# Batch 2's additions of weighted values: from VectorE to GpSimd

## The chip, the cores and the metric

The kernel runs on one core of a Trainium2 chip. The metric is the device time in microseconds of one execution, as a median over runs; the profile is of one further execution. Engines are named as in the profile: PE is TensorE, DVE is VectorE, ACT is ScalarE, POOL is GpSimd, SP is SyncE, whose queue here issues most transfers.

## The reference

Four sequences (batches 0 to 3) of 512 tokens, width 256, all in float32. The first layer is a cross attention over 1,024 context tokens with 16 heads of 16. The second is a block that attends, for each token, over the batches, and then runs a mixture of experts. Cut to what matters here, with the third-batch step marked:

```python
x = x + xattn(layernorm(x), ctx, ctx, mask, ...)          # 4 x 512 x 256
hidden = layernorm(x)
qkv = einsum('sbh,oh->sbo', layernorm(hidden) * w1 + b1, qkv_weight)   # 16 heads of q, 4 of k and v
scores = einsum('sbhd,tbhd->bhst', q, k) * 0.25
probs = softmax(where(causal, scores, min))
attn = einsum('bhst,tbhd->sbhd', probs, v)                # <- the sum over t
h2 = hidden + attn @ proj_weight.T
gate = softmax(layernorm(h2) @ router_weight.T)           # top 2 of 8 experts
out = x + h2 + sum over the two chosen experts of gate * gelu(. @ w1) @ w2
```

The block's first axis, over which it attends causally, is what the first layer calls the batch. So token s of batch b attends to token s of batches 0 to b: for batch 2 the sum over t has three terms, each a weighted copy of one batch's values.

## The kernel before

**Stages.** First come some 28 us of loading and preparation, then to about 637 us the cross attention of 16 groups (4 batches by 4 groups of 4 heads), with the second layer's work on batches 0, 1 and 2 spread between its steps, and then the experts' tiles (39 of them) with batch 3's second layer between them.

**Cross attention.** A group takes 8 steps. In each step TensorE forms score products twice: `psm` (L1147), from which DVE takes maxima, `mx` (L1154), ten steps ahead, and `pss` (L1168), from which ACT takes exponentials, `ex` (L1176). `ex` meets the values in `av` (L1186), which a group sums in one PSUM bank over its 8 steps. At the end of a group DVE's transposition to `oraw` (L862) empties that bank, so the next group's first `av` waits for it. `divide` then makes `rec` and `on` (L875, L876) and every second time `onT` (L862).

**Second layer.** `half(b, h)` is a generator that does two of the four 128-token tiles of batch b, one piece at a time; pieces end at a `yield`. For batch 2, in order: variances and their power on POOL (L268); normalised rows `hn` (L434, DVE); `hT`; `q`, `keys`, `values` (L455 to L458); POOL's products `pr` of q with the keys of batches 0, 1 and 2 (L489); sums, maxima and exponentials in `sc` (L500 to L509); then one piece with the weighted values: POOL writes batch 0's product into `at` and those of batches 1 and 2 into `pr[:, 1]` and `pr[:, 2]` (L514; the profile calls this buffer `pv`), and two additions put them onto `at` (L532). That piece ends, and at least two steps later the transposes `psa` (L294) read `at`, followed by `aT`, `psp` (L542), `h2` (L549), statistics, `vm` (L555), its power `rm` on POOL, `xt` on POOL (L557), Newton's step `sm`, `sm`, `rm` (L274 to L276) and `rows` (L562) on DVE, the transposes `psx`, and the router.

**Order.** The order of instructions is written out: each engine runs its own instructions in the order in which the program issues them, and one that waits holds all behind it on that engine. Which step a piece falls into is decided by a planner from costs given with each piece (`PARTS`); those costs don't depend on the engine that line 532 names. Buffers of the step: `at` and `pr` have one buffer each for batches 0 to 2, all in SBUF, float32, 128 x 512 a piece.

Line 532 names DVE for batch 2 and POOL for batch 1. Batch 0 has nothing to add, and batch 3 sums with one reduction (L525) instead.

Of the kernel before, what the change touches and what calls it, by code (L numbers as in the profile page):

```python
# [10 lines left out]
ALU = mybir.AluOpType  # L11
# [162 lines left out]
def kernel(  # L174
# [21 lines left out]
    nc = tc.nc  # L196
# [207 lines left out]
    def products_of(name, b):  # L404
        if b < B - 1:
            return k2.tile([P, B - 1, HALF, DK], F32, tag="pr", name=name, bufs=1)
        return late["pool"].tile([P, B, HALF, DK], F32, tag="prlast", name=name, bufs=2)
# [6 lines left out]
    def half(b, h):  # L414
# [47 lines left out]
        def of_batch(kv, j):  # L462

            return (
                kv[j][:, t0 : t0 + 2, :]
                .rearrange("p t (k d) -> p (t k) d", d=DK)
                .unsqueeze(2)
                .to_broadcast([P, 2 * KVH, REP, DK])
            )

        def grouped(x):
            return x.rearrange("p (k r) d -> p k r d", r=REP)

        if b == 0:

            yield
            yield
            yield
            at = k2.tile([P, HALF, DK], F32, tag="at", name=f"at{n}", bufs=1)
            nc.gpsimd.tensor_copy(grouped(at), of_batch(values, 0))  # L480
            yield
        else:

            def engine(j):
                return nc.vector if last and j % 2 else nc.gpsimd

            pr = products_of(f"pr{n}", b)
            for j in range(b + 1):
                engine(j).tensor_tensor(  # L489
                    grouped(pr[:, j]),  # L490
                    grouped(q.rearrange("p i (h d) -> p (i h) d", d=DK)),
                    of_batch(keys, j),
                    ALU.mult,
                )
            yield "D1.5|G2.4"
            sc = k2.tile([P, B, HALF], F32, tag="sc", name=f"sc{n}")[:, 0 : b + 1, :]
            top = k2.tile([P, HALF], F32, tag="top", name=f"top{n}")
            by_head = sc.rearrange("p j n -> p n j")
            over = [P, b + 1, HALF]
            nc.vector.tensor_reduce(sc, pr[:, 0 : b + 1], AX.X, ALU.add)  # L500
            nc.vector.tensor_reduce(top, by_head, AX.X, ALU.max)
            nc.vector.tensor_tensor(sc, sc, top.unsqueeze(1).to_broadcast(over), ALU.subtract)
            if last:
                yield "D3!"
            nc.scalar.activation(sc, sc, AF.Exp, scale=SCALE)
            yield "A2.9"
            nc.vector.tensor_reduce(top, by_head, AX.X, ALU.add)
            nc.vector.reciprocal(top, top)
            nc.vector.tensor_tensor(sc, sc, top.unsqueeze(1).to_broadcast(over), ALU.mult)  # L509
            yield "D1"  # L510
            at = k2.tile([P, HALF, DK], F32, tag="at", name=f"at{n}", bufs=1)
            pr = products_of(f"pv{n}", b)
            for j in range(b + 1):
                engine(j).tensor_tensor(  # L514
                    grouped(pr[:, j] if j or last else at),
                    of_batch(values, j),
                    sc[:, j, :]
                    .rearrange("p (k r) -> p k r", r=REP)
                    .unsqueeze(3)
                    .to_broadcast([P, 2 * KVH, REP, DK]),  # L520
                    ALU.mult,
                )
            if last:
                yield "D1.5|G2.4"
                nc.vector.tensor_reduce(  # L525
                    at.rearrange("p n d -> p (n d)"),
                    pr.rearrange("p j n d -> p (n d) j"),
                    AX.X,
                    ALU.add,
                )  # L530
            for j in range(1, 1 if last else b + 1):
                (nc.vector if b == 2 else nc.gpsimd).tensor_tensor(at, at, pr[:, j], ALU.add)  # L532
            yield "D2.2!"
        aT = wide(f"aT{n}")
        rows_of = at.rearrange("p (i h) d -> p i (h d)", i=2)
# [349 lines left out]
    def project_o(b, t):  # L885
# [9 lines left out]
        nc.vector.tensor_tensor(xt[:, b, t, :], ps[:, 0:D], xt[:, b, t, :], ALU.add)  # L895

    halves = {(b, h): half(b, h) for b in range(B) for h in range(2)}

    with ExitStack() as actx:
# [35 lines left out]
        for h in range(H):  # L935

            g, j = divmod(h, 4)
# [776 lines left out]
```

## Time and profile before

| | us |
|---|---|
| Median of 3 runs (836.19 to 838.76) | 836.48 |
| The profiled execution's own time | 840.55 |
| Its span, first to last instruction | 838.8 |
| Mean granted TensorE clock | 0.985 |
| DVE's four instructions of L532: shortest, median, longest | 0.692, 0.898, 1.529 |
| POOL's two instructions of L532 (batch 1): shortest, longest | 1.268, 1.273 |
| POOL's product `at` of L514: shortest, longest | 1.043, 1.053 |
| POOL's `xt` of L557, an addition of the same size: mean | 1.266 |
| DVE's `on` of L876: shortest, median, longest | 0.424, 0.425, 1.232 |

Each row of a timeline has the start in the span, the length, the engine, the line, the operation, the output and input by the program's names, their shapes, and how many instructions were merged into the row. In square brackets stands how long the engine had been idle before it, and what ended that. A granted clock of 0.5 means that TensorE ran at half its full speed. Windows give the busy time of each engine in a stretch. Batch 2's two halves reach line 532 at 584.6 us and 611.1 us.

### The profile page before, as it was taken

The numbers are of one execution on the slowest core, as the hardware profiler recorded it, in microseconds if no ns is written. First come the engines' busy times: TensorE is split into PE (matmuls) and PEld (weight loads), VectorE is DVE, ScalarE is ACT, GpSimd is POOL, SyncE is SP. The second block draws the span as 40 slices with busy tenths as digits, with TensorE's granted clock in tenths as the row PEclk, the third lists the DMA queues.
The fourth block names the chain that finished last, engine by engine and source line by source line (L and its number), as shares of the span: only waits on it lengthen the run. The fifth ranks groups of instructions, "written<-read, shape, count | busy, mean of one in ns | idle before, by whom it ended". The sixth has DMA issues, their size and how long they took to land.

```text
span 838.8 us, 14851 instructions
## 1 busy us (share of the span) xinstructions
PE 791.9 (94%) x5255; PEld 409.2 (49%) x5255; DVE 561.7 (67%) x1335; ACT 441.9 (53%) x896; POOL 290.0 (35%) x445
## 2 busy tenths in 40 slices
PE   5999999999999999999999999999989989789993
PEld 4553433333433333444433333433326878789992
DVE  5687667666778777887786878888845587501033
ACT  2326666655565656555655565555555665434441
POOL 6815351001353300154653201223223564525531
PEclk9999999999999999999999999999989999989997
DMA  7229203408000000000000006000071450278954
GB/s 234 60 92 312 63 1 109 126 1 233 2 26 1 1 1 2 1 27 27 2 1 1 1 1 202 27 20 8 1 254 58 141 190 20 78 241 268 342 175 152
DMA packets 55641, 73.36 MB, mean 87 GB/s; under 512 B 5721, under 2 KB 40569, under 8 KB 55568
## 3 DMA queue, kind: packets, MB, share of 16 engines
q1 hardware_dynamic: 49968, 61.08, 23.8%
q0 software_dynamic: 4080, 10.07, 3.3%
q10 hardware_dynamic: 1520, 1.27, 0.5%
q8 instruction: 42, 0.69, 0.3%
q14 instruction: 31, 0.25, 0.1%
HBM read 42.88 MB, written 30.75 MB: 88 GB/s over the span
## 4 chain that ended last, share of the span: by engine, by line
PE 69%; DVE 11%; issue 10%; POOL 7%; DMA 1%; ACT 1%; POOLq 0%; ACTq 0%; SPq 0%; DVEq 0%
PE psm L1147 29%; PE av L1186 13%; PE psv L1061 4%; POOL given_rows L1483 4%; PE psk L1028 3%; DVE mx L1154 3%; PE pss L1168 3%; PE psq L448 2%; PE psp L542 2%; PE psy L1469 2%; PE psqt L1127 2%; PE pskt L1049 2%; PE psp L888 2%; PE psu L1451 2%; PE psq L1107 1%
## 5 line engine op out<-in xcount | busy, mean ns | idle before, releaser
L1154 DVE TENSOR_REDUCE mx<-psm 128x1 f32<-128x512 f32 x512 | 326.1, 683 | 115.2 <-PE pss L1168 100.7
L1176 ACT ACTIVATE ex<-pss 128x512 f32<-128x512 f32 x512 | 277.4, 596 | 203.6 <-PE pss L1168 192.4
L1147 PE MATMUL psm<-kT_odd,shared 32*128 32x512 f32 x512 | 152.1, 639 | 3.1 <-ACT shared L1135 2.1
L1168 PE MATMUL pss<-qt,shared 32*128 32x512 f32 x512 | 151.6, 639 | 0.0
L1168 PE MATMUL pss<-qt,kT_odd 32*128 32x512 f32 x512 | 146.5, 646 | 0.9 <-ACT ex L1176 0.9
L1147 PE MATMUL psm<-shared 32*128 32x512 f32 x512 | 143.0, 639 | 0.7 <-ACT shared L1135 0.7
L1186 PE MATMUL av<-ex,vaug 128*32 128x512 f32 (+1 forms) x888 | 107.1, 551 | 4.4 <-DVE sm L274 4.1
L1451 PE MATMUL psu<-shared 128*128 128x128 f32 x624 | 78.2, 277 | 2.9 <-ACT shared L1436 2.4
L993 POOL TENSOR_TENSOR shared<-shared 128x256 f32<-128x256 f32 x44 | 33.5, 761 | 135.0 <-ACT shared L1036 113.6
L1147 PEld LDWEIGHTS psm<-kT_odd,shared 32*128 32x128 f32 x512 | 43.8, 183 | 74.3 <-DVE mx L1154 33.8
L1451 PEld LDWEIGHTS psu<-shared 128*128 128x128 f32 x624 | 76.6, 193 | 6.9 <-ACT shared L1436 4.0
L1469 PE MATMUL psy<-shared 128*128 x312 | 77.6, 393 | 1.1 <-issue 0.6
L1147 PEld LDWEIGHTS psm<-shared 32*128 32x128 f32 x512 | 42.3, 183 | 65.5 <-DVE mx L1154 29.2
L1469 PEld LDWEIGHTS psy<-shared 128*128 128x128 f32 x312 | 58.0, 196 | 9.4 <-issue 1.7
L1186 PEld LDWEIGHTS av<-ex,vaug 128*32 128x32 f32 x888 | 17.8, 108 | 89.2 <-issue 81.2
L1460 ACT ACTIVATE shared<-psu 128x512 f32<-128x512 f32 x39 | 23.4, 599 | 49.2 <-PE psu L1451 22.7
L1168 PEld LDWEIGHTS pss<-qt,kT_odd 32*128 32x128 f32 x512 | 42.8, 184 | 8.3 <-ACT ex L1176 3.8
L995 POOL TENSOR_TENSOR shared<-shared 128x128 f32<-128x128 f32 x88 | 44.8, 530 | 0.0
L1168 PEld LDWEIGHTS pss<-qt,shared 32*128 32x128 f32 x512 | 43.6, 183 | 2.0 <-ACT ex L1176 1.5
L268 POOL TENSOR_TENSOR rm<-vm,power 128x2 f32<-128x2 f32 x8 | 5.7, 712 | 109.4 <-DVE vm L555 87.0
L653 POOL DMA_INDIRECT table<-rows,index x32 | 32.4, 1013 | 31.9 <-issue 11.4
L1515 DVE SCALAR_TENSOR_TENSOR y<-y,gate,xt 128x256 f32<-128x256 f32 x16 | 7.7, 481 | 45.9 <-DMA y<-given_rows 45.9
(296 smaller groups left out, 1041.4 us busy)
## 6 DMA issues: line engine op xcount, KB each, us to landing
shared<-in_moe_w_dram SPq DMA_DIRECT2D x47, 512.0 KB
table<-zeros SPq DMA_DIRECT2D x8, 2120.0 KB
shared<-in_ctxT_dram SPq DMA_DIRECT2D x8, 512.0 KB
y<-given_rows SPq DMA_DIRECT2D x12, 256.0 KB
shared<-table SPq DMA_DIRECT2D x18, 132.5 KB
xt<-in_x_dram SPq DMA_DIRECT2D x4, 512.0 KB
rows_d<-table SPq DMA_DIRECT2D x13, 132.5 KB
out_dram<-y SPq DMA_DIRECT2D x6, 256.0 KB
```

What stands on the lines that cost most here:

```text
L653: inst = nc.gpsimd.indirect_dma_start(out=table, out_offset=bass.IndirectOffsetOnAxis(ap=index, axis=0), in_=rows, in_offset=None, bounds_ ...
L993: engine.tensor_tensor(a, src, over(f[:, 0:DK]), ALU.mult)
L995: engine.tensor_tensor(r[:, :, i::2], src[:, :, 1 - i :: 2], over(f[:, DK + i : 2 * DK : 2]), ALU.mult,)
L1061: nc.tensor.matmul(ps[:, 0:D], context(b, kc, c), wv_sb[:, c, :], start=(c == 0), stop=(c == KC - 1),)
L1147: nc.tensor.matmul(ps, q1[m][rows, t * P : (t + 1) * P], kT[b % 2][rows, g, h * 512 : (h + 1) * 512], start=True, stop=True,)
L1154: nc.vector.tensor_reduce(mx[m][:, t, j, h : h + 1], ps, AX.X, ALU.max)
L1168: nc.tensor.matmul(ps, kT[b % 2][rows, g, kc * P : (kc + 1) * P], q2[m][rows, :], start=True, stop=True,)
L1176: nc.scalar.activation(ex[m, kc, j], ps, AF.Exp, scale=SCALE)
L1186: nc.tensor.matmul(av[m][32 * j : 32 * j + 32, over], vaug[(b * NKC + kc) % VRING][:, 4 * g + j, :], x[:, over], start=(kc == 0), stop=(kc ...
L1451: nc.tensor.matmul(ps_of[k][:, of], w1_of[k][:, c, of], xT_of[k][:, c, :], start=(c == 0), stop=(c == KC - 1),)
L1469: nc.tensor.matmul(ps_of[k], h_of[k][:, f * P : (f + 1) * P], w2_sb[:, bass.ds(weights_of[k] + f * D, D)], start=(f == 0), stop=(f == F // ...
L1483: inst = nc.gpsimd.indirect_dma_start(out=given_rows[n], out_offset=bass.IndirectOffsetOnAxis(ap=number[name][:, i, :], axis=0), in_=y, in ...
```

## The change

Line 532 chose the engine by the batch. Now it always takes POOL, which also writes the three products that are added. So for batch 2, four additions of 128 x 512 float32 (two in each half) go from DVE's queue to POOL's, right behind the products of line 514. Nothing else differs: the planner's costs, the steps of the pieces, the buffers and all other instructions are as before, and DVE has no instruction left in that piece.

```diff
@@ half(b, h)
             for j in range(1, 1 if last else b + 1):
-                (nc.vector if b == 2 else nc.gpsimd).tensor_tensor(at, at, pr[:, j], ALU.add)
+                nc.gpsimd.tensor_tensor(at, at, pr[:, j], ALU.add)
             yield "D2.2!"
```

## The prediction

> **What bounds the kernel now.** I read the page first, then the answer for line 532, then the timeline around its four VectorE instructions, the chain of waits there, and windows of TensorE's clock.
>
> The page says TensorE is the engine that sets the span, but that is an average: the change touches four instructions of batch 2, so what counts is which wait ends last near 585 and 611 us.
>
> ```profile
> span 838.8 us, 14851 instructions
> PE 791.9 (94%) x5255; PEld 409.2 (49%) x5255; DVE 561.7 (67%) x1335; ACT 441.9 (53%) x896; POOL 290.0 (35%) x445
> ```
>
> The answer for line 532 shows the moved instructions (four on DVE), the same addition already on POOL for batch 1 (1.27 us each), and one long DVE wait.
>
> ```profile
> L532 DVE TENSOR_TENSOR at<-at,pv x4: 692/898/1529, 584.6 to 612.7; 128x512 f32<-128x512 f32 x4
> L532 POOL TENSOR_TENSOR at<-at,pv x2: 1268/1270/1273, 447.8 to 476.0; 128x512 f32<-128x512 f32 x2
> ...
>   POOL pv L514: 4.1, 1
> ```
>
> Timeline, half (2, 0): start, length, engine, line.
>
> ```profile
> 583.06 2.06 POOL L514 TENSOR_TENSOR pv<-values,sc 128x512 f32<-128x512 f32 x2
> 584.56 1.90 DVE L532 TENSOR_TENSOR at<-at,pv 128x512 f32<-128x512 f32 x2
> 586.61 3.90 POOL L489 TENSOR_TENSOR pr<-q,keys 128x512 f32<-128x512 f32 x3 [1.49 <-DVE keys L457]
> 586.92 1.23 DVE L876 TENSOR_TENSOR on<-oraw,rec 128x256 f32<-128x256 f32 x1
> 588.83 2.44 DVE L1154 TENSOR_REDUCE mx<-psm 128x1 f32<-128x512 f32 x4
> 589.53 0.69 PE L1147 MATMUL psm<-kT_odd,shared 32*128 32x512 f32 x1 [0.96 <-DVE mx L1154]
> ```
>
> DVE works without a pause; the chain of waits runs down DVE from 583.38 to the variance `vm` at 606.98, and TensorE waits 0.96 us for it. So DVE is the bound here, not TensorE. Half (2, 1):
>
> ```profile
> 607.06 0.72 POOL L268 TENSOR_TENSOR rm<-vm,power 128x2 f32<-128x2 f32 x1 [16.55 <-DVE vm L555]
> 607.77 1.26 POOL L557 TENSOR_TENSOR xt<-xt,h 128x512 f32<-128x512 f32 x1
> 609.00 1.04 POOL L514 TENSOR_TENSOR at<-values,sc 128x512 f32<-128x512 f32 x1
> 610.01 2.05 POOL L514 TENSOR_TENSOR pv<-values,sc 128x512 f32<-128x512 f32 x2
> 611.09 2.33 DVE L532 TENSOR_TENSOR at<-at,pv 128x512 f32<-128x512 f32 x2 [4.11 <-POOL pv L514]
> 613.33 0.71 DVE L862 STREAM_TRANSPOSE oraw<-av 128x512 f32<-128x512 f32 x1
> 614.09 1.94 PE L1186 MATMUL av<-ex,vaug 128*32 128x512 f32 x8 [4.08 <-DVE sm L274]
> 615.96 1.12 PE L294 MATMUL psa<-ident,at 128*128 128x128 f32 x4
> ```
>
> Here DVE stands 4.11 us at the first addition, and `oraw`, which frees the bank that the next `av` products need, stands behind it in DVE's order; so TensorE stands 4.08 us. Its clock drops (columns PE, PEld, DVE, ACT, POOL busy, then granted clock, DMA share, GB/s):
>
> ```profile
> 608.00:614.00 6.00, 2.01 (x16) 0.34 (x12) 2.81 (x4) 4.13 (x8) 4.06 (x4) 0.82 0.66 210
> 614.00:620.00 6.00, 5.91 (x29) 1.72 (x30) 1.73 (x8) 1.56 (x4) 0.00 (x0) 0.61 0.90 272
> ```
>
> In half-microsecond windows it is 0.50 from 611.8 to 618.7, so 4.6 us of work from 614.09 run at half speed: some 2.3 us lost.
>
> **The change, first half.** It takes 1.90 us from DVE at 584.56. Only 0.69 + 0.69 is work; the rest is DVE held until POOL's current instruction ends: the first addition ends at 585.67, the products at 585.12. `on` shows the same: 1.23 us beside POOL's `pr`, against a median of 0.42. POOL gets two additions of 1.27 with 0.08 before each (the gap after the product in batch 1: 447.71 to 447.79): 585.20 to 586.47 and 586.55 to 587.82. DVE goes on to `keys` once ACT's copy of `q` ends (584.87 + 0.37 = 585.24), then `values` and `rec`, and reaches `on` near 585.8. It is held to the end of the first addition, 586.47, and ends 0.27 later (as before: POOL's first `pr` ended at 586.61 + 1.27 = 587.88, `on` at 588.15). So 586.74 instead of 588.15: DVE is **1.4 us** early, and as the chain is DVE's alone to 606.98, all that follows is too: TensorE, which waited for `mx` at 589.53, moves by as much. Ends for it: 0.1, if `on` gets through only after both additions (587.82 + 0.27 = 588.09); 1.9, if all the addition time is saved. I take 1.4, by the row of `on`, which got its turn with two `pr` instructions still to come.
>
> What waits for POOL now: the three `pr` behind the additions start 587.9 instead of 586.61 and end by 591.8. Line 500 wants them at 600.05 - 1.4 = 598.6: 6.8 us of cover. `psa` of this half stood at 593.64, less 1.4 is 592.2, against 587.82: 4.4 us of cover. Both would cost, microsecond for microsecond, only beyond that. SP's queue has nothing of this step, and the step issues no DMA.
>
> **Second half**, first in the old times. POOL's row is `rm`, `xt`, three products, which end at 612.06, then additions 612.14 to 613.41 and 613.49 to 614.76. Meanwhile DVE no longer stands: `av` of the old product ends at 608.94, `oraw` at 609.7, the `ex` that the next `av` reads at 610.08, so `av` runs at 610.1 to 611.2 instead of 614.09 to 616.03. Then TensorE meets `psa`, which needs the additions: the stall moves from `oraw` to `at`. DVE's `sm`, `sm`, `rm`, two `rows` and `on` now fall beside POOL's products and additions. What this costs POOL: at 253.5 to 257.1 eight such short DVE instructions, `hn` (0.41 alone, 0.6 to 0.9 there) among them, lay beside POOL's and left those at their usual lengths; three `pr` took 3.90 beside `on` against 3.73 without. I take 0.15. Ends: 0, and 2.0, if each of the two later products and two additions grows by the 0.45 to 0.51 that the longest rows show in batch 3 (1.50 against 1.04, 1.77 against 1.26). So `psa` comes at 614.76 + 0.15 + 0.05 (step from engine to engine) = 614.96 instead of 615.96: **1.0 us** early, and with the 1.4 before it 2.4. DVE's `rows` are needed by `psx` only after `psa`, `pss` and `av`, over 2 us later; late by more, they would hold that. Behind POOL's additions its next instruction is `rm` at 628.8: 14 us of cover.
>
> **The clock** is the third term. TensorE's stall is now 611.2 to 614.96, 3.8 us against 4.08, with dense work before and after. Before, the clock fell 1.8 us after the stall began. I count the same 2.3 us lost, difference 0; ends +2.3 gained (no drop) and 1.1 lost (all 6.8 us of the slow stretch fall on work: 3.4 - 2.3).
>
> The Trainium skill ("TensorE: Matmul & The Clock Gate", "HAM oscillation") has idle gaps above some 3.4 us halve the clock, by a free-running window; the trace's drop, 1.8 us into a gap, doesn't need a whole idle window. By the page a gap of 3.8 us would mostly escape, and the sum would be 831.8; by the row it is 834.1.
>
> The Trainium skill ("SBUF — State Buffer", "Who interferes with whom") speaks against the change: a VectorE instruction with two SBUF inputs and a GpSimd one that reads SBUF exclude each other, whoever comes second waiting for the whole instruction. The held `on` agrees; GpSimd's unlengthened rows at 254 to 258 us don't. If POOL waited for all 1.7 us of those DVE instructions, the sum would be 835.6 and not 834.1.
>
> **Sum.** After 616 us TensorE is busy without a gap to 638, then the experts and batch 3 hang on its results; the rows read for the first tiles were asked for from 607.5 to 623.7 and are used from 637, so DMA doesn't absorb the gain, and the 6.6 us wait for rows of the last list near 734 follows DVE's and POOL's work. So 840.55 (the profiled execution, span 838.8) less 2.4 gives 838.15; that execution lies 4.07 above the median of the runs, so for the median 836.48 - 2.4 = **834.1**. Own range 832.9 to 835.4.
>
> **Rivals.**
> - *No cold clock* in the second half: 834.1 - 2.3 = 831.8. For it: the stall is shorter and split from the one before by `av`. Against: by 0.3 us only.
> - *The first half gives nothing*: `on` is held through both additions, gain 0.1 + 1.0 = 1.1, so 835.4. For it: POOL's additions follow without a wait. Against: `on` slipped in between two `pr`.
> - *Slower*: POOL pays for the port. At line 532 of half (2, 1), POOL's four instructions grow to 2.0 us more, `psa` comes at 616.81, 0.85 late; less 0.1 from the first half, and with up to 1.1 of cold clock on top: 837.2 to 838.3. It decides from the point where POOL's lengthening exceeds the first half's gain by 1.15. For it: batch 3's rows. Against: those stand beside DVE instructions of 0.69 us, here they are mostly 0.16.
> - *It doesn't do what it says*: excluded, since the trace has this very line on POOL in batch 1.
>
> **How the numbers follow.** Forecast 0.56, no cold clock 0.15, first half nothing 0.16, slower 0.13. 0.3% is 2.5 us, about what a measurement of this kernel can tell. Faster than 833.97 are a little under half of the forecast, whose middle lies 0.1 us above that (0.27), the clock case (0.15) and a clock gain on top of the second rival (0.02): 0.44. Slower than 838.99 needs the slower case and more: 0.10. The rest, 0.46, is within. The range 831.6 to 836.9 reaches to the clock case and leaves most of the slower one out.
>
> **What would show it.** Line 532 has six POOL rows of 1.27 and none on DVE; `on` of half (2, 0) ends 1.4 us earlier after POOL's products than now; no DVE wait of 4 us near 611; `av` runs before `psa` with the stall between them; `psa` follows POOL's last addition within 0.1 us. I am wrong if `psa` stands later relative to `vm` than 9.0 us (now 615.96 - 606.98), if POOL's additions take over 1.6 us, or if the 2.4 us gained by 616 are gone at 742.

## The result, and the profile after

| | before | after |
|---|---|---|
| Median of 12 runs each, us | 837.32 (834.66 to 838.80) | 839.49 (837.19 to 841.66) |
| Ratio of times | | 1.0032 [1.0020, 1.0044] |
| Profiled execution, us | 840.55 | 840.89 |
| Its span, us | 838.8 | 839.0 |
| Mean granted TensorE clock | 0.985 | 0.981 |

The change made the kernel slower by 0.32% by the ratio, about 2.7 us (the two medians lie 2.2 apart). 834.1 had been forecast, 2.4 us below the 836.48 of the runs known then, in a range of 831.6 to 836.9. The table's last three rows already hold a hint: the two profiled executions differ by 0.3 us only, and by the clock.

The page of the changed kernel: DVE lost four instructions, POOL got four, and POOL's busy time rose by 4.9 us.

```profile
span 839.0 us, 14850 instructions
PE 792.5 (94%) x5255; PEld 409.6 (49%) x5255; DVE 563.2 (67%) x1331; ACT 442.0 (53%) x896; POOL 294.9 (35%) x449
```

DVE's line speaks: four instructions worth 4 us are gone, yet it is busy 1.5 us *longer*. Other DVE instructions became slower, in both halves. The answer for line 532 shows the edit in place, six instructions on POOL of 1.25 to 1.34 us, and who waits for them:

```profile
L532 POOL TENSOR_TENSOR at<-at,pv x6: 1252/1270/1336, 448.1 to 616.3; 128x512 f32<-128x512 f32 x6
...
  PE psa L294: 3.5, 1
```

**First half of the change**, the timeline of DVE, POOL and TensorE around it, in the changed kernel:

```profile
583.72 1.05 POOL L514 TENSOR_TENSOR at<-values,sc 128x512 f32<-128x512 f32 x1 [13.36 <-DVE sc L509]
584.73 2.06 POOL L514 TENSOR_TENSOR pv<-values,sc 128x512 f32<-128x512 f32 x2
586.75 2.69 POOL L532 TENSOR_TENSOR at<-at,pv 128x512 f32<-128x512 f32 x2
587.77 0.53 DVE L876 TENSOR_TENSOR on<-oraw,rec 128x256 f32<-128x256 f32 x1
588.97 2.45 DVE L1154 TENSOR_REDUCE mx<-psm 128x1 f32<-128x512 f32 x4
589.51 3.73 POOL L489 TENSOR_TENSOR pr<-q,keys 128x512 f32<-128x512 f32 x3
591.34 0.70 DVE L693 SCALAR_TENSOR_TENSOR lna<-base,base 128x8 f32<-128x8 f32 x1
592.07 1.31 DVE L682 TENSOR_TENSOR gea<-lna,full 128x128 f32<-128x128 f32 x1
594.54 2.48 DVE L1154 TENSOR_REDUCE mx<-psm 128x1 f32<-128x512 f32 x4
595.37 0.63 PE L294 MATMUL psa<-ident,at 128*128 128x128 f32 x4 [1.65 <-DVE mx L1154]
```

And the same instructions in the kernel before:

```profile
582.05 1.05 POOL L514 TENSOR_TENSOR at<-values,sc 128x512 f32<-128x512 f32 x1 [12.00 <-DVE sc L509]
...
591.20 0.14 DVE L693 SCALAR_TENSOR_TENSOR lna<-base,base 128x8 f32<-128x8 f32 x1
591.38 0.29 DVE L682 TENSOR_TENSOR gea<-lna,full 128x128 f32<-128x128 f32 x1
...
592.82 2.47 DVE L1154 TENSOR_REDUCE mx<-psm 128x1 f32<-128x512 f32 x4
593.64 0.63 PE L294 MATMUL psa<-ident,at 128*128 128x128 f32 x4 [0.18 <-DVE mx L1154]
```

`lna` and `gea` belong to a piece that plans the list of rows for the first expert tiles. They have nothing to do with the second layer; they only happen to come next on DVE. In the old kernel POOL's three `pr` were over at 586.61 + 3.90 = 590.51, and `lna` came 0.69 us behind them. Now the two additions stand ahead of `pr`, which run from 589.51 to 593.24, and `lna` and `gea` fall among them. `lna` takes 0.70 in place of 0.14 and `gea` 1.31 in place of 0.29: together **1.58 us**, as much as DVE had been relieved of. The maxima `mx` behind them are late, and TensorE, which stood 0.18 us at `psa`, stands 1.65.

All of this timeline lies some 1.7 us later than in the old profile for a reason of its own: POOL's first product `at` starts at 583.72 and not 582.05, behind a stretch at half clock near 580 that comes before the first changed instruction. So intervals are compared here, not places: the products end at 586.79 and `on` at 588.30, 1.51 apart, where it was 585.12 to 588.15, 3.03 apart.

**What the stall brings.** Windows of the changed kernel (start:end length, busy time and instructions of PE, PEld, DVE, ACT and POOL, granted clock, DMA share, GB/s):

```profile
590.00:596.00 6.00, 4.35 (x46) 1.62 (x38) 5.79 (x13) 2.87 (x6) 3.24 (x3) 1.00 0.00 1
596.00:602.00 6.00, 6.00 (x28) 2.02 (x28) 4.72 (x17) 2.57 (x5) 0.00 (x0) 0.72 0.01 3
```

The first of them in the kernel before:

```profile
590.00:596.00 6.00, 5.82 (x48) 2.10 (x48) 5.70 (x19) 3.46 (x7) 0.51 (x1) 1.00 0.02 4
```

TensorE is busy 4.35 of 6 us in place of 5.82, and in the next 6 us the clock is 0.72: it is 0.50 from 596.1 to 599.5 and 1.00 after. TensorE has work throughout (6.00 busy), so the 3.41 us at half clock cost half of that, 1.7 us. All stretches at half clock that the profiles of this case show are 3.41 us long, or two or three times that, but for the last, which begins near 830 us and runs past the end. Their mean number in an execution, in units of 3.41 us, can therefore be read from its mean clock: (1 - clock) x span / 1.7. For the changed kernel's 12 runs that gives 8.2; for the before runs beside the experiments below, 6.2 to 6.7.

**Second half**, in the changed kernel:

```profile
609.99 0.72 POOL L268 TENSOR_TENSOR rm<-vm,power 128x2 f32<-128x2 f32 x1 [16.75 <-DVE vm L555]
...
611.96 0.72 DVE L862 STREAM_TRANSPOSE oraw<-av 128x512 f32<-128x512 f32 x1 [2.05 <-PE av L1186]
...
612.82 1.24 PE L1186 MATMUL av<-ex,vaug 128*32 128x512 f32 x8
613.03 0.98 DVE L275 TENSOR_TENSOR sm<-sm,rm 128x2 f32<-128x2 f32 x1
...
614.96 2.59 POOL L532 TENSOR_TENSOR at<-at,pv 128x512 f32<-128x512 f32 x2
615.05 2.65 DVE L562 TENSOR_SCALAR rows<-h,mvm,rm 128x256 f32<-128x256 f32 x2
...
617.61 1.11 PE L294 MATMUL psa<-ident,at 128*128 128x128 f32 x4 [3.55 <-POOL at L532]
...
620.67 1.94 PE L1186 MATMUL av<-ex,vaug 128*32 128x512 f32 x8
```

This went as forecast: no DVE wait of 4 us, `av` before `psa`, the stall between them, `psa` 0.06 us behind POOL's last addition. From the start of `rm` to `psa` are 7.62 us, where it was 615.96 - 607.06 = 8.90: 1.28 us less. But where the `av` of the old kernel took 1.94 us, all of it at half clock (1.07 at full), now an `av` *behind* the stall takes 1.94, and the one before it 1.24. In this execution the slow stretch was moved, not removed.

### The profile page after: what moved, and what is told of

It is laid out like the page before. It is cut to its first block, busy times and chain, and to the rows that moved or that the text cites. A ratio compares the mean times of both kernels' runs of the same rounds, so it can differ in the third digit from the quotient of the medians.

```text
span 839.0 us, 14850 instructions
## 1 busy us (share of the span) xinstructions
PE 792.5 (94%) x5255; PEld 409.6 (49%) x5255; DVE 563.2 (67%) x1331; ACT 442.0 (53%) x896; POOL 294.9 (35%) x449
## 3 DMA queue, kind: packets, MB, share of 16 engines
q10 hardware_dynamic: 1520, 1.27, 0.5%
## 4 chain that ended last, share of the span: by engine, by line
PE 69%; DVE 9%; issue 8%; POOL 6%; DMA 3%; SPq 2%; ACT 2%; ACTq 0%; POOLq 0%; DVEq 0%
PE psm L1147 29%; PE av L1186 14%; PE psv L1061 4%; PE psk L1028 3%; PE pss L1168 3%; POOL given_rows L1483 3%; DVE mx L1154 2%; PE psq L448 2%; PE psp L542 2%; PE pskt L1049 2%; PE psqt L1127 2%; PE psp L888 2%; PE psu L1451 2%; PE psq L1107 1%; PE psy L1469 1%
```

## The experiments

The theory at the outset: the first half's gain is taken back by `pr` falling on `lna` and `gea`, and the stall this makes brings half clock. Rivals: the second half costs more than it saves; the two sets of runs differ by chance; the half clock is the whole loss and has nothing to do with the stall at `psa` of half (2, 0).

All ratios are to the kernel before, run alternately on the same chip. "Half-clock stretches" are means over an execution, counted as above.

**Before, unchanged**, to see what no change looks like.

> The kernel before under another label, so that its own runs, with their mean granted clocks, stand beside those of the others. All theories: no difference beyond 0.1%. If the time of single runs goes with the granted clock, a run whose mean clock is 0.004 lower should be some 3 us longer.

Measured: 837.15 us, 1.0006 [0.9996, 1.0015], 6.4 half-clock stretches. The loss of 0.32% is five times this difference, and a second set of the changed kernel, further down, is slower too, so chance between sets is not the reason. Among single runs the time does go with the clock: a line through these 12 runs gives 2.6 us for 0.004 of mean clock, one through the 35 before runs beside them 1.8, where 3 had been expected. So a stretch in the count costs some 0.9 to 1.3 us on average, less than 1.7, since not every stretch lies on work.

**One half of the change alone.** On the kernel before:

```diff
-(nc.vector if b == 2 else nc.gpsimd).tensor_tensor(at, at, pr[:, j], ALU.add)
+(nc.vector if b == 2 and h == 1 else nc.gpsimd).tensor_tensor(at, at, pr[:, j], ALU.add)
```

moves the first half's alone; with `h == 0` in place of `h == 1` the second half's alone.

> Additions on POOL in half (2, 0) only. Collision theory (POOL's pr of the next half comes 1.3 us later and then stands beside DVE's lna and gea, which take 1.6 us more): slower by 1 to 3 us, with lna and gea near 0.7 and 1.3 us. Rival (the moved stall before psa in half (2, 1) costs the time): same as before or 1.4 us faster. Rival (chance of the clock windows): no difference.

> Additions on POOL in half (2, 1) only. Collision theory: faster by about 1 us (psa follows vm after 7.7 us and not after 9.0), lna and gea at 0.14 and 0.29 us. Rival (the moved stall before psa costs the time, by a longer slow clock): slower by 1 to 3 us. Rival (chance): no difference.

Measured: first half alone 839.49, 1.0023 [1.0008, 1.0037], 7.5 stretches; second half alone 836.90, 1.0001 [0.9991, 1.0012], 6.5. The loss is the first half's; the rival that puts it on the second falls. The one profile of the first half alone caught a mild case: `lna` took 0.58 and `gea` 0.29, since `gea` got in between two of POOL's instructions, and TensorE stood 0.6 at `psa`. So the same kernel was run once more:

> The first-half-only kernel again. Slower than before by 0.1 to 0.35%. If the loss comes by slow windows: mean clock lower than before's by 0.002 or more, the rest of the time within 0.5 us of before's.

Measured: 838.35, 1.0015 [1.0001, 1.0029], 7.0 stretches, and this time the whole picture:

```profile
590.07 0.69 DVE L693 SCALAR_TENSOR_TENSOR lna<-base,base 128x8 f32<-128x8 f32 x1
590.79 1.32 DVE L682 TENSOR_TENSOR gea<-lna,full 128x128 f32<-128x128 f32 x1
```

with a wait of 1.8 us at `psa`, and in the windows half clock directly behind it:

```profile
589.00:595.40 6.40, 4.64 (x42) 1.85 (x40) 6.20 (x13) 2.89 (x6) 2.96 (x3) 1.00 0.00 1
595.40:599.00 3.60, 3.60 (x18) 0.79 (x18) 3.15 (x14) 1.20 (x2) 0.00 (x0) 0.56 0.02 5
```

The second half alone shows why its gain of 1.28 us comes to nothing in the time. Its windows, split where the clock falls:

```profile
609.00:615.50 6.50, 3.01 (x23) 0.98 (x20) 5.84 (x8) 3.59 (x8) 5.99 (x6) 1.00 0.75 229
615.50:619.00 3.50, 3.50 (x19) 0.75 (x17) 0.34 (x1) 1.72 (x4) 0.00 (x0) 0.53 0.95 285
```

The stretch at half clock lies wholly on work (3.50 busy of 3.50), where in the profile of the kernel before it began during the stall. A fair interval runs from the power `rm` of half (2, 0) to the same `rm` of half (2, 1), compared between profiles with the same number of half-clock stretches inside. With one stretch it is 21.20 to 21.22 us with the additions on DVE (three profiles) and 20.79 to 20.87 on POOL (three profiles): 0.4 us gained, not 1.0. With none, in runs with filled stalls below, 19.65 against 19.25: again 0.4. With two it is 21.76 to 21.86 on DVE (three profiles, the kernel before among them) and 21.89 and 22.12 on POOL (the change, and the change with its first stall filled): nothing gained. There the pair began some 2.2 us before the stall's end in the old order, and 0.6 to 1.0 before it in the new, so more of it fell on work. A ratio known to 0.1% can't tell 0.4 us from nothing.

**The colliding piece one step later.** If the theory holds, the changed kernel with `lna` and `gea` out of the way must keep the first half's gain. In the planner's steps, on the changed kernel and, for what the move does by itself, on the kernel before:

```diff
 steps = plan.spread(START, END)
+lists_at = [T for T in range(START, END) for f, args in steps[T] if args[:1] == (first_list,)]
+piece = [s for s in steps[lists_at[0]] if s[1][:1] == (first_list,)][0]
+steps[lists_at[0]].remove(piece)
+steps[lists_at[0] + 1].insert(0, piece)
```

> The changed kernel, with the first piece of the list's planning (lna, gea and the six small instructions behind them on DVE) put one step later, behind the next four maxima. Collision theory: lna and gea at 0.14 and 0.29 us, and faster than before by 1 to 3 us. Rival (stall before psa): still slower than before by about 2 us, as the change is. Rival (chance): no difference.

> The kernel before, with only the planning piece put one step later as in the list-later run. Collision theory: lna and gea are short in both, so within 0.7 us of before. Rival (the later piece is a gain of its own, whatever the additions do): faster than before by 1 to 2 us, as the list-later run was against the change.

Measured: changed kernel with the piece later 836.05, 0.9987 [0.9974, 1.0001], 7.3 stretches; the kernel before with it 839.32, 1.0010 [0.9996, 1.0024], 6.7. In the first, `pr` were over at 592.86, and then:

```profile
593.89 0.16 DVE L693 SCALAR_TENSOR_TENSOR lna<-base,base 128x8 f32<-128x8 f32 x1
594.09 0.29 DVE L682 TENSOR_TENSOR gea<-lna,full 128x128 f32<-128x128 f32 x1
```

Out of POOL's way they take 0.16 and 0.29, as in the kernel before (0.14 and 0.29), and the loss is gone; the later place brings the kernel before nothing. No stretch follows `psa` of half (2, 0) in this profile. But the count of 7.3 is above the 6.2 of the before runs beside it: the loss went without a lower count, and where those stretches lie in the other executions is open. The interval that tells it best runs from POOL's first product of half (2, 0) to `rm` of that half, through DVE's whole chain: 25.01 us before (582.05 to 607.06) and 24.16 here (583.34 to 607.50). With the piece later and the additions on DVE it was 25.70; with the piece later and the additions on POOL, 24.17 in the filled run below. So against the same place of the piece the first half is worth 1.5 us, close to the 1.4 forecast.

**POOL later, additions left where they were.** On the kernel before, two instructions of like length on POOL behind `pr`:

```diff
+if (b, h) == (2, 1):
+    nothing = named["zeros"][:, 0:1].unsqueeze(2).to_broadcast([P, HALF, DK])
+    for _ in range(2):
+        nc.gpsimd.tensor_tensor(pr[:, 0], pr[:, 0], nothing, ALU.add)
```

> The kernel before (all four additions on DVE), with two more POOL additions of zero onto one piece of pr behind the three pr products of half (2, 1): the result stays the same, POOL stays busy 2.5 us longer, to about 593. Collision theory: lna and gea take about 0.7 and 1.3 us and not 0.14 and 0.29, and the kernel is slower than before by 1.5 to 3.5 us, with no addition moved. Rival (the loss lies in what the moved additions themselves do): within 0.5 us of before.

Measured: 839.39, 1.0012 [0.9998, 1.0026], 6.6 stretches: some 1 us slower, less than the collision theory expected and more than its rival did. The expected collision hardly came about:

```profile
591.37 2.29 POOL L498 TENSOR_TENSOR pr<-pr,zeros 128x512 f32<-128x512 f32 x2
592.09 0.34 DVE L697 SCALAR_TENSOR_TENSOR lna<-base,base 128x8 f32<-128x8 f32 x1
592.47 0.29 DVE L686 TENSOR_TENSOR gea<-lna,full 128x128 f32<-128x128 f32 x1
```

`lna` waited 0.2 us, and `gea` slipped in ahead of the second instruction of POOL; only a later one, `lha` at 593.11, took 0.57 in place of 0.17. This run decides nothing, except that how long DVE is held depends on where within POOL's instruction it arrives.

**The stalls filled.** If half clock follows TensorE's stalls, transposes whose result nobody reads, put into a stall, should keep the clock up and change nothing else. Into the stall at `psa` of half (2, 1), in the changed kernel and in the one with the piece later:

```diff
-def transposed(dst, src, name, weight=None):
+def transposed(dst, src, name, weight=None, fill=0):
...
+    for _ in range(fill):
+        nc.tensor.transpose(ps[:, 0:P], ident, ident)
...
+fill = 20 if (b, h) == (2, 1) else 0
-transposed(aT, lambda i: rows_of[:, i, :], f"psa{n}")
+transposed(aT, lambda i: rows_of[:, i, :], f"psa{n}", fill=fill)
```

> The changed kernel, with 20 transposes of the identity (3.1 us at full clock) into psa's bank ahead of its own transposes in half (2, 1): TensorE works through its stall. If the slow clock behind this stall is part of the loss: one to two slow windows of 3.4 us fewer there, mean clock up by 0.002 to 0.004, 1.5 to 3.5 us faster than the change. If the collision alone is the loss: no faster than the change by more than 0.5 us.

> The changed kernel with the planning piece one step later and the 20 transposes in the stall. If both terms are real and add up: 832 to 834.5 us, faster than before by 2 to 4 us. If the clock term is not real: about the list-later run, 836.

Measured: the change filled 837.39, 0.9986 [0.9970, 1.0003], 5.8 stretches; with the piece later too 836.44, **0.9969 [0.9958, 0.9981]**, 6.1 stretches, by its ratio the fastest version of all here, on a chip whose before runs had a median of 838.68 and 6.7 stretches. The transposes took 2.40 us, so that TensorE still stood 1.19 at `psa`. The clock holds, in the changed kernel filled:

```profile
610.00:616.00 6.00, 4.81 (x40) 2.77 (x36) 5.52 (x6) 3.44 (x7) 5.87 (x6) 1.00 0.72 236
616.00:622.00 6.00, 6.00 (x44) 2.43 (x44) 1.17 (x4) 4.23 (x9) 0.00 (x0) 1.00 0.81 256
```

That it pays in the old order too is shown by the kernel before with its own stall filled, ahead of the first `av` of the last group, which waits for its bank:

```diff
 av[m] = pso.tile(...)
+if m == M - 1:
+    work = pss.tile([P, 512], F32, tag="s", name="work")
+    for _ in range(22):
+        nc.tensor.transpose(work[:, 0:P], ident, ident)
```

> The kernel before, with 22 transposes of the identity (3.5 us) into a score bank ahead of the first av of the last group, where TensorE stands 4.1 us. If the slow clock behind this stall cost the kernel before as much as I put it at (2.3 us): 1.5 to 2.5 us faster than before. If the stall's slow clock is a cost of the change alone: no difference.

Measured: 835.67, 0.9983 [0.9973, 0.9992], 1.4 us and so a little less than expected, 6.0 stretches, and a clock of 1.00 where the kernel before had 0.61:

```profile
614.00:620.00 6.00, 4.45 (x35) 1.61 (x34) 3.49 (x10) 1.89 (x5) 0.00 (x0) 1.00 0.89 263
```

One thing here doesn't fit well. With the second half's stall filled in both, the change (0.9986) and the kernel before (0.9983) are equal within their intervals, though the first half's stall is not filled in either. By the plain change's 1.0018 to 1.0032 some 0.2 to 0.3% should have been left; put the other way, this fill brought the change 0.3 to 0.5%, and the kernel before 0.17. The intervals, on two chips, are too wide to exclude 0.2%.

**The stall that the change made, filled.** The sharpest test of the last rival: transposes into the stall at `psa` of half (2, 0), which leave the collision alone, beside the plain change on the same chip.

```diff
+if (b, h) == (2, 0):
+    work = pss.tile([P, 512], F32, tag="s", name="work")
+    for _ in range(10):
+        nc.tensor.transpose(work[:, 0:P], ident, ident)
 transposed(aT, lambda i: rows_of[:, i, :], f"psa{n}")
```

> The changed kernel, with 10 transposes of the identity (1.6 us) into a score bank ahead of psa in half (2, 0), where TensorE stood 1.65 us behind the delayed maxima. If the slow window at 596 us is part of the loss in most executions: none there, mean clock up by 0.001 to 0.002, 0.8 to 1.7 us faster than the change. If that window was one execution's chance: as the change, within 0.5 us.

> The changed kernel once more, beside the others of this call. Slower than before by 0.2 to 0.45%, some two slow clock windows more per execution than before (mean clock lower by 0.003 to 0.004). Its profile shows lna and gea near 0.7 and 1.3 us again, psa 7.7 us behind vm, and whether 596 us has a slow window again.

Measured: filled 837.32, 1.0000 [0.9990, 1.0009]; plain 839.13, 1.0018 [1.0007, 1.0028]. So the slow clock behind this one stall is 0.18% of the time, 1.5 us (by the single times of the two sets the 95% interval of the difference is 0.5 to 2.6 us), which is the whole loss of this set. The collision stays in the filled run:

```profile
589.70 0.69 DVE L697 SCALAR_TENSOR_TENSOR lna<-base,base 128x8 f32<-128x8 f32 x1
590.42 1.31 DVE L686 TENSOR_TENSOR gea<-lna,full 128x128 f32<-128x128 f32 x1
```

but the clock doesn't fall behind it (the transposes took 1.31 us, and TensorE still stood 0.51 at `psa`):

```profile
590.00:596.00 6.00, 5.49 (x50) 2.68 (x46) 5.71 (x15) 2.73 (x6) 1.59 (x2) 1.00 0.01 4
596.00:602.00 6.00, 6.00 (x40) 2.35 (x39) 5.79 (x15) 1.71 (x4) 0.00 (x0) 1.00 0.00 0
```

The mean number of half-clock stretches is 6.7 against 7.8 for the plain change on the same chip, and 6.3 for the kernel before. The profiles say the same in the interval from POOL's first product of half (2, 0) to `rm`:

| | us | stretches at half clock inside |
|---|---|---|
| additions on DVE, planning piece in its place (four profiles) | 25.00 to 25.36 | none |
| on POOL, full collision: stall filled; only the later stall filled | 25.07; 25.07 | none |
| on POOL, full collision: the change; first half again | 26.27; 26.43 | one |
| on POOL, full collision: the change again | 27.82 | two |
| on POOL, piece later (two profiles) | 24.16, 24.17 | none |

With the clock held, what the first half saves on DVE and what `lna` and `gea` lose are equal; a slow stretch adds 1.2 to 1.4 us. The second row's latter run had nothing put into this stall, so it isn't the transposes that bring 25.07.

## Why the prediction was wrong, step by step

**What held.** Six POOL rows of 1.27 and none on DVE. `on` 1.5 us earlier against POOL's products (1.51 behind them, 3.03 before; 1.4 forecast). No 4 us wait on DVE, `av` ahead of `psa`, `psa` 0.06 us behind the last addition, and 617.61 - 609.91 = 7.70 us behind `vm`, where more than 9.0 would have been wrong. The rival in which POOL pays for the port did not come: the two additions beside DVE's `rm` and `rows` took 2.59 together, next to twice 1.27.

**The step that failed: "What waits for POOL now".** It asked who needs the delayed `pr`, found line 500 with "6.8 us of cover" and `psa` with 4.4, and put the delay at nothing. Both covers were real. But `pr` is also a neighbour. It ran 1.23 us later behind POOL's products (2.72 in place of 1.49) while DVE ran 1.5 earlier, so the two engines moved some 2.6 us against one another, and `lna`, which had come 0.69 us after the end of `pr` (591.20 - 590.51), now came 1.90 ahead of it (593.24 - 591.34). Price 1.58 us, which is the whole of the "**1.4 us** early". That it is this is shown by the piece moved one step on (durations back to 0.16 and 0.29, 1.5 us of gain in the interval), and by the two runs in which the collision is full and no slow clock follows (25.07 us, no gain left). The prediction had used this very mechanism for the old `on`, and missed it in the place to which it was moved.

The Trainium skill ("SBUF — State Buffer", "Who interferes with whom") has a VectorE instruction with two SBUF inputs locked out for the whole GpSimd instruction that it meets, and the other way round. DVE's side agrees with `lna` (0.14 to 0.70) and `gea` (0.29 to 1.31); POOL's side shows little, with 2.59 for two additions.

**The clock term, "difference 0", with ends +2.3 and -1.1.** It looked at one stall, the second half's. There the rival without a slow clock didn't come: in all five profiles with the additions on POOL and that stall unfilled, a stretch began in it or up to 0.8 us behind it. But the first half made a new one, 1.65 us at `psa`, and the clock fell behind it in three of the four profiles that had the full collision and no fill there (the change, the change again, the first half again; not in the change with only the later stall filled). Its price is 1.5 us by the runs with and without the fill, and no term of the prediction held it: the end of 1.1 lost was for the other stall. The 2.3 us charged to the old order's slow clock were 1.4 [0.7, 2.3] by the fill there.

**The second half, "1.0 us early": mis-sized, at most 0.4 was left.** `psa` did come 1.28 earlier, but the old place of `psa`, 615.96, held some 0.87 us that `av` had lost to half clock (1.94 in place of 1.07). Where no slow clock touched that `av`, in the kernel before with the piece later, the old order has `psa` at 616.63 - 608.60 = 8.03 behind `rm`, and 8.03 - 7.62 is 0.41. The prediction charged the slow stretch to the old order, kept it unchanged in the clock term, and took its end of `psa` from a row without it. The slow stretch then fell on later work, and where it was a double one, as in the changed kernel's own profile, the 0.4 went with it.

**The sum.** From -2.4: the first half's 1.4 given back and the second half's 0.6 too much make -0.4; the new slow stretch adds 1.5: +1.1. Measured were 1.0032, some +2.7, in the first set and 1.0018 [1.0007, 1.0028], +1.5, in the second: the sum lies within the second interval and below the first one. The rest, 0.4 to 1.6 us, is not accounted for; up to 0.8 of it may be the second half, which with a double stretch lost its 0.4 and up to 0.4 more. The half-clock count of the first set (8.2, against 7.8 when it was run again) is higher too, but why is open, and so is how often the stall brings two stretches, as in one profile of the change run again, and not one.

**Not tried.** The piece later and the fill in the kernel before, which would say what the change is worth on top of both; and `lna` and `gea` in a form that reads only one input from SBUF.

## What to carry to other kernels

When work is moved to GpSimd, don't ask only who waits for what is behind it: lay the later instructions beside VectorE's new times and look for those with two SBUF inputs that will now meet them, down to the smallest, since here 0.14 us of work was held for 0.56. Ask of every new wait on TensorE, even one under 2 us, what the clock does behind it, and don't count a gain up to an instruction that lies in or just behind a stretch at half clock. To tell a stall from its clock, fill it with transposes that nobody reads; here that was worth 0.17 and 0.18% in the two stalls where it was tried alone.

## What the runs showed of the hardware

- Half the clock after a short stall. TensorE waited 1.65 to 1.8 us, was busy in 4.35 of 6 us around it (the changed kernel), and then ran at 0.50 for 3.41 us or twice that, in three of four profiles. The Trainium skill ("TensorE: Matmul & The Clock Gate", "HAM oscillation") has gaps above some 3.4 us as the ones that bring the slow clock; the length of the slow stretch agrees with its 3.4, the length of the gap doesn't.
- Where the stall lies seems to count. Within each profile the stretches start whole multiples of 3.41 us apart (579.0, 596.1 and 616.6 in the change). Laid out as a grid, the stall of half (2, 0) lies almost wholly in one step of 3.41 us in the three profiles in which the clock fell behind it, with TensorE busy for 1.76, 1.68 and 1.71 us of that step; in the one in which it didn't, the grid parts the stall, with 2.04 and 3.03 us busy in the two steps. Four profiles suggest this, they don't show it, and the busy time alone is not the rule: at 688.2 to 691.6 us of the change TensorE was busy 1.71 of 3.40, and the clock held.
- How long DVE is held is not set by its own size: `lna`, 128 x 8, grew by 0.56 us, `gea`, 128 x 128, by 1.02, and in another run `gea` beside POOL's work kept its 0.29, having come between two POOL instructions. `rec` and `onT`, which read one array, kept 0.24 and 0.71 beside `pr` in the kernel before.
- The meeting is lopsided. In the second half, DVE's `sm` of 128 x 2 elements took 0.98 us and the two `rows` 2.65 (0.16 and 0.74 for the same ones in the kernel before), held by POOL's instructions, while POOL's two additions there took 2.59, next to twice 1.27. That DVE time lay beside a stall of TensorE, and no wait of TensorE for it shows.
